# Moving a projection ahead of a transpose, a value projection one step back, a table's second part into two places, and dropping one warm-up product

## Chip, cores and metric

The kernel runs on one core of one Trainium2 chip, as one program. The metric is the device time of the whole execution in microseconds. Three runs of the kernel before gave 546.41, 546.90 and 547.14 us, so the median is 546.90 us.

## The reference, cut to what matters

Everything is float32. There are 8 batches of 256 tokens with 256 features each, and each batch has a context of 120 rows.

```python
# 16 heads of 64; x: (8, 256, 256), context: (8, 120, 256)
q = (layernorm(x) @ w_q);  k, v = context @ w_kv          # 256 -> 1024 each
attn = softmax(q @ k^T / 8)                               # per batch and head, 256 x 120
x = x + tanh(g_xattn) * ((attn @ v) @ w_out + b_out)
# mixture of experts: 8 experts, 256 -> 1024 -> 256, each token goes to its best 2
logits = layernorm(x) @ Wr^T;  gate = top-2 of softmax(logits), divided by their sum
x = x + tanh(g_ffn) * sum_e gate_e * (silu(layernorm(x) @ W1_e^T) @ W2_e^T)
```

## The kernel before, in words

**Order.** The instruction streams of TensorE (PE), VectorE (DVE), ScalarE (ACT) and SyncE (SP) run in the order in which the program text issues them (`tc.manual_schedule`); only GpSimd (POOL) is ordered by a planner. Each engine takes its stream from the front, so an instruction that waits holds up all that is written behind it on the same engine.

**Attention, lines 1067 to 1163.** A loop goes over 32 steps `s`. Step `s` is batch `b`, half of the heads `o`, and half of the tokens `nb`; `k = 2*o + nb` counts the four steps of a batch, and `n = b + 1` is the next batch. In each step the program issues, in this order:

- `scores(s+1)`: 16 small matmuls into `psc` (one pair of PSUM banks, used again by every step), the maximum `mx` on DVE, and eight exponentials on ACT that read `psc`;
- products for this and the next batch: `weigh` (`po`, attention times v), `project_q` (`pq`), `project_v` (`pv`, copied out by ACT), `wide_out` (`pw`), and k for later batches, `project_k` for batch 1 and `project_kk` for two batches at once (`pk`, copied to `kT` by DVE). They take turns in the four PSUM banks of `ps_mm`;
- on DVE the copies of `pk`, and then `divide(s+1)`, the division by the softmax sum;
- in steps with routing the `router`, some twenty short DVE instructions on a 128 by 32 block, with one exponential (L265) on ACT near its start;
- `turn_pr(s)`: eight PE transposes of the divided probabilities into `tr`, copied to `pT_sb` by ACT (L584). The next step's `weigh` reads `pT_sb`.

**Routing in the attention.** When `b` is 3 or 5, the step `k = 1` also computes the logits of the two batches finished before. `logits` issues 16 products into `plT`, a DVE copy to `lgT` (L227), and after a `yield` the PE transpose of `lgT` into `pl` (L230), which the router reads. In step `k = 1` the program issues `plT`, then `project_q`, then that transpose, then `wide_out`, and last `project_kk`. Batch 7 has its own order for this, which is not touched.

**Experts, lines 1182 to 1271.** A loop goes over 31 tiles of 128 rows. Tile `i` issues `go_up` (32 matmuls of `ph`), `open_tile(i+1)` (for gathered tiles a DVE copy of that expert's first weights, L834; then two transposes and the DVE copy `xT`, L856), then on DVE `w2_of()` (for gathered tiles the copy of the second weights, L843), then `close_tile` (16 matmuls `py` of tile `i-1` and its scaling `y` on DVE, L887). The scaled rows are added to the output by an indirect DMA of POOL (L904). The first eight tiles use an expert's weights in place; from tile 8 on, a table built on the chip says which rows and which expert a tile has. That table is the generator `table()`: a first part at `i = 4`, then at `i = 5` the part that gives rows and experts of full tiles (lines 728 to 733, used by the row loads of SP), and at the end of `i = 5` the part for quarter tiles (lines 736 to 782), which also gives `more_i`, a count that every engine loads into a register at `i = 8` (L1198) and that guards a branch at `i = 12` (L1185).

**Start.** Eleven products that nobody reads (`idle`, lines 1048 to 1050) run on PE until the first normalised rows are there.

Of the kernel before, what the change touches and what calls it, by code (L numbers as in the profile page):

```python
# [16 lines left out]
B, N, D = 8, 256, 256  # L17
# [31 lines left out]
def tile_gated_xattn_moe(  # L49
# [232 lines left out]
    def count(n, pool):  # L282

        pc = pool.tile([P, 512], F32, tag="mm", name=f"pc_{n}")
        nc.tensor.matmul(
            pc[:, :E], lhsT=ones, rhs=tally[:, n, :], start=True, stop=True
        )
        return pc[:, :E]
# [202 lines left out]
    def project_kk(b, h):  # L491
# [15 lines left out]
            pk[:, : 4 * M],  # L507
        )

    def project_q(b, xnT, h):  # L510
        pq = ps_mm.tile([P, 2, N], F32, tag="mm", name=f"pq_{b}_{h}")
        for i in range(2):
            for c in range(DC):
                nc.tensor.matmul(  # L514
                    pq[:, i, :],
                    lhsT=wq_sb[:, c, ts(2 * h + i, P)],
                    rhs=xnT[:, c, :],
                    start=(c == 0),
                    stop=(c == DC - 1),
                )  # L520
        nc.scalar.copy(qT_sb[b % 2][:, ts(h, 2), :], pq)

    def project_v(b, j):
        pv = ps_mm.tile([P, 512], F32, tag="mm", name=f"pv_{b}_{j}")
        for c in range(DC):
            nc.tensor.matmul(
                pv[:M, :],
                lhsT=ctxT_sb[:, c, ts(b, M)],
                rhs=wkv_sb[:, c, ds(INNER + j * 512, 512)],
                start=(c == 0),  # L530
                stop=(c == DC - 1),
            )
        nc.scalar.copy(v_sb[b % 2][:, ts(j, 512)], pv[:M, :])
# [152 lines left out]
    def where(first, used, dst):  # L686

        nc.vector.tensor_scalar(first, first, -float(NOWHERE), None, ALU.add)
        nc.vector.tensor_tensor(first, first, used, ALU.mult)
        nc.vector.tensor_scalar(dst, first, float(NOWHERE), None, ALU.add)  # L690
# [8 lines left out]
    def table():  # L699

        rest_i = row("rest_i", E, I32)
        nc.vector.scalar_tensor_tensor(
            rest_i, count(NBLK, fw[2]), float(-P), bump, ALU.add, ALU.add
        )
        whole_i = row("whole_i", E, I32)
        nc.vector.tensor_scalar(whole_i, rest_i, 7, None, ALU.arith_shift_right)
        counts, begin = row("counts", 2 * E), row("begin", 2 * E)
        tails, whole = counts[:, :E], counts[:, E:]  # L710
        nc.vector.tensor_scalar(whole, whole_i, 1.0, None, ALU.mult)
        left = row("left", E)
        nc.vector.scalar_tensor_tensor(
            left, whole, float(-P), rest_i, ALU.mult, ALU.add
        )
        nc.vector.tensor_scalar(tails, left, float(P - QUARTER), None, ALU.is_gt)
        nc.vector.tensor_scalar(begin[:, E:], first_row, float(P), None, ALU.add)
        nc.vector.scalar_tensor_tensor(
            begin[:, :E], whole, float(P), begin[:, E:], ALU.mult, ALU.add
        )  # L720
        upto = summed("w", counts)

        at = row("at", FULLS)
        nc.vector.tensor_scalar(at, places_w, upto[:, 2 * E - 1 :], None, ALU.add)
        used = row("used_w", FULLS)
        nc.vector.tensor_scalar(used, at, 0.0, None, ALU.is_ge)
        yield
        which, first = sought("w", at, upto, counts, begin, P)
        full_row = row("full_row", FULLS, I32)
        where(first, used, full_row)  # L730
        expert_i = row("expert_i", FULLS, I32)
        nc.vector.tensor_scalar(used, which, float(E), float(-E), ALU.is_ge, ALU.mult)
        nc.vector.tensor_tensor(expert_i, which, used, ALU.add)
        yield expert_i, full_row

        quarters = row("quarters", E)
        nc.vector.tensor_scalar(quarters, left, 0.0, None, ALU.is_gt)
        for k in range(1, 3):
            nc.vector.scalar_tensor_tensor(
                quarters, left, float(k * QUARTER), quarters, ALU.is_gt, ALU.add  # L740
            )
        nc.vector.scalar_tensor_tensor(
            quarters, tails, -3.0, quarters, ALU.mult, ALU.add
        )
        upto_q = summed("q", quarters)
        used = row("used_q", 5 * QUADS)
        nc.vector.tensor_scalar(used, places_q, upto_q[:, E - 1 :], None, ALU.is_lt)
        which, first = sought("q", places_q, upto_q, quarters, begin[:, :E], QUARTER)
        where(first, used, first)
        nc.vector.tensor_scalar(which, which, float(E - 1), None, ALU.min)  # L750

        quad_row = row("quad_row", QUADS, I32)
        nc.vector.tensor_scalar(quad_row, first[:, :QUADS], lane, None, ALU.add)
        own = row("own", QUADS * E).rearrange("p (n e) -> p n e", e=E)
        eighth = row("eighth", QUADS)
        nc.vector.tensor_scalar(
            eighth, which[:, :QUADS], -1.0, float(E), ALU.mult, ALU.add
        )
        shape = [P, QUADS, E]
        nc.vector.tensor_tensor(  # L760
            own,
            rank.unsqueeze(1).to_broadcast(shape),
            eighth.unsqueeze(2).to_broadcast(shape),
            ALU.is_equal,
        )
        octets = which[:, QUADS:].rearrange("p (n e) -> p n e", e=E)
        nc.vector.tensor_tensor(
            octets, octets, octal.unsqueeze(1).to_broadcast([P, QUADS // 2, E]), ALU.mult
        )
        experts_i = row("experts_i", QUADS // 2, I32)  # L770
        with nc.allow_low_precision("whole numbers under 2**24, exact"):
            nc.vector.tensor_reduce(experts_i, octets, AX.X, ALU.add)

        more, more_i = row("more", 1), row("more_i", 1, I32)
        nc.vector.tensor_scalar(
            more, upto[:, 2 * E - 1 :], float(SPARE - FULLS), 0.0, ALU.add, ALU.max
        )
        more_q = row("more_q", 1)
        nc.vector.tensor_scalar(
            more_q, upto_q[:, E - 1 :], float(-4 * MIXED), 0.0, ALU.add, ALU.max  # L780
        )
        nc.vector.tensor_tensor(more_i, more, more_q, ALU.add)
        yield quad_row, own, experts_i, more_i

    tables = []
# [260 lines left out]


    idle = ps_tr.tile([P, 4, P], F32, tag="tr", name="idle")
    for _ in range(11):
        nc.tensor.matmul(idle[:, 0, :], lhsT=ones, rhs=before, start=True, stop=True)  # L1050


# [4 lines left out]
    for h in range(2):  # L1057
        project_q(0, xnTs[0], h)
# [8 lines left out]
    for s, (b, o, nb) in enumerate(units):  # L1067
        k = 2 * o + nb
        n = b + 1
# [17 lines left out]
        copies, sums = [], []  # L1087
# [8 lines left out]
                sums.append(wide_out(b - 1, 1, ps_mm))  # L1096
        if k == 0:
            project_q(b, xnTs[b], 3)
            project_v(b, int(b == 0))
        elif n < B:  # L1100
            project_q(n, xnTs[n], k - 1)
        if k == 1:
            if b == 0:
                copies.append(project_k(1, 0))
            if routing and n < B:
                lg = next(lg)
            if b > 0:
                sums.append(wide_out(b - 1, 0, ps_mm))
            if routing and n == B:
                lg = next(lg)  # L1110
        if k == 3:
            if b == 0:
                copies.append(project_k(1, 1))
            if b > 0:
                project_v(b, 1)

        if b == 1:
            copies.append(project_kk(2, k))
        elif 1 < b < 6 and k % 2 == 1:
            copies.append(project_kk(2 * (b // 2) + 2, 2 * (b % 2) + k // 2))  # L1120
        for copy in copies:
            copy()
        if s + 1 < len(units):
# [58 lines left out]
    for i, t in enumerate(order):  # L1182
        if i == 12:

            with tc.If(more > 0):  # L1185
# [8 lines left out]
                    for _ in quad(j, load(("quad", j))):  # L1194
                        pass
                spare = None
        if i == 8:
            more = nc.values_load(tables[1][3][0:1, 0:1], min_val=0, max_val=FULLS)  # L1198
        w2_of = state["ready"][2][2]
        if i == 2:  # L1200
# [12 lines left out]
        copies = []  # L1213
# [10 lines left out]
            open_tile(order[i + 1], xts[i + 1])  # L1224
        if mixed:
            next(running)
        if i == 5:
            tables.append(next(parts))
        if i == 0:
            norms_y.finish()  # L1230
            weigh(B - 1, 1, ps_py)
            load_expert(4)
            turn_y(B - 2, bank_tr)
            sending[g - 1] = places(g - 1, groups[g - 1][0], picked[g - 1], bank_tr)
# [18 lines left out]
        if i == 4:  # L1253
            parts = table()
# [4 lines left out]
                    tc.tile_pool(name="quads", bufs=1, side="right", reuse_waits="tile")  # L1259
                )  # L1260
            )
        if i == 5:
            tables.append(next(parts))
        while len(xts) <= min(i + AHEAD, len(order) - 1 if tables else 7):
            xts[len(xts)] = load(order[len(xts)])
        if i == mix - 4:
# [48 lines left out]
```

## Time and profile before

| what | value |
|---|---|
| median of three runs | 546.90 us |
| the profiled execution, its own time | 546.83 us |
| its span, first to last instruction | 545.1 us |
| mean granted TensorE clock | 0.995 |
| PE busy | 528.0 us, 97% of the span |
| PE weight loads busy | 445.5 us, 82% |
| DVE, ACT, POOL busy | 282.5, 219.6 and 128.7 us |

The busy time of PE runs to a modelled end of each matmul, and matmuls overlap: eight products of `pq` are listed as 1.99 us, but the next group starts 1.83 us after them when nothing is late. So waits of PE are best read as the distance between the starts of two groups, against the same distance elsewhere in the trace. In a list of waits the first number is the idle time of the waiting engine, behind the name of what it waited for. In a timeline the columns are the start, the length, the engine, the line, the operation, the tile written and those read, the shape, the number of instructions merged in the row, and in brackets the idle time just before and what ended it.

### The profile page before, as it was taken

What the parts mean: (1) busy time and instruction counts of PE and PEld (TensorE: products, weight loads), DVE (VectorE), ACT (ScalarE), POOL (GpSimd) and SP (SyncE); (2) the same over time, 40 slices, a digit from 0 to 9 for tenths busy, and PEclk for the clock granted to TensorE, in tenths of its full rate; (3) what the DMA queues carried; (4) which work ended last, traced back from release to release, by engine and by line L of the source; (5) the groups of instructions that cost most, each with busy time, mean ns of one, the idle gap of its engine ahead of it and who ended that gap; (6) DMA issues with size and microseconds to landing.
All of it is one profiled execution on the core that took longest, in us unless ns stands there. A gap on an engine that the chain in (4) does not pass through costs nothing. (4 is left out here: it accounts for less than half of the span.)

```text
span 545.1 us, 9935 instructions
## 1 busy us (share of the span) xinstructions
PE 528.0 (97%) x3700; PEld 445.5 (82%) x3700; DVE 282.5 (52%) x683; ACT 219.6 (40%) x700; POOL 128.7 (24%) x135
## 2 busy tenths in 40 slices
PE   8999999998999999999999999999999999999992
PEld 7788887877878777786789998998997887889991
DVE  3675545664775548655573348344443354443530
ACT  1666546473564634757630310111143645601110
POOL 2011100000332001320003564112331124233422
PEclk9999999999999999999999999999999999999998
DMA  8999991230340500112079932222221220321321
GB/s 298 334 283 280 281 279 44 68 126 2 111 143 30 186 1 20 42 41 59 2 266 321 351 82 71 40 39 34 41 39 31 30 43 6 52 40 15 45 26 19
DMA packets 46439, 57.53 MB, mean 106 GB/s; under 512 B 3184, under 2 KB 41456, under 8 KB 46384
## 3 DMA queue, kind: packets, MB, share of 16 engines
q1 hardware_dynamic: 39488, 47.35, 29.3%
q0 software_dynamic: 6480, 8.81, 9.2%
q8 instruction: 32, 0.52, 0.4%
q10 hardware_dynamic: 416, 0.66, 0.4%
q14 instruction: 23, 0.19, 0.1%
HBM read 28.67 MB, written 28.27 MB: 104 GB/s over the span
## 5 line engine op out<-in xcount | busy, mean ns | idle before, releaser
L564 ACT ACTIVATE pr<-psc,mx 128x120 f32<-128x120 f32 x256 | 88.4, 372 | 69.8 <-DVE mx L558 64.6
L863 PEld LDWEIGHTS ph_full<-xT_full,w 128*128 128x128 f32 x736 | 85.1, 192 | 6.4 <-issue 5.7
L863 PE MATMUL ph_full<-xT_full,w 128*128 128x128 f32 x736 | 86.8, 276 | 0.3 <-PEq L1185 0.3
L879 PE MATMUL py_full<-w,hT_full 128*128 128x256 f32 x368 | 83.1, 379 | 0.0
L879 PEld LDWEIGHTS py_full<-w,hT_full 128*128 128x128 f32 x368 | 68.2, 190 | 8.4
L904 POOL DMA_INDIRECT out_dram<-y_full,xt_full x23 | 40.2, 1746 | 100.8 <-DVE y_full L887 71.8
L514 PE MATMUL pq<-xnT,w_sb 128*128 128x256 f32 x256 | 62.7, 388 | 0.4 <-DVE xnT L207 0.4
L871 ACT ACTIVATE hT_full<-ph_full 128x1024 f32<-128x1024 f32 x23 | 23.5, 1023 | 97.7 <-PE ph_full L863 97.7
L608 PE MATMUL pw<-w_sb 128*128 128x256 f32 x256 | 58.5, 382 | 0.0
L564 ACT ACTIVATION_READ_ACCUMULATOR pr<-psc,mx 128x1 f32 x256 | 55.6, 217 | 0.0
L514 PEld LDWEIGHTS pq<-xnT,w_sb 128*128 128x128 f32 x256 | 46.6, 190 | 10.8 <-issue 1.9
L608 PEld LDWEIGHTS pw<-w_sb 128*128 128x128 f32 x256 | 47.8, 190 | 8.9 <-DVE mx L558 0.8
L552 DVE TENSOR_REDUCE mx<-psc 128x8 f32<-128x960 f32 x32 | 36.8, 1151 | 21.8 <-PE psc L544 21.6
L365 POOL DMA_INDIRECT routed<-rows,slot x32 | 32.2, 1006 | 52.6 <-DVE slot L361 45.6
L584 ACT COPY w_sb<-tr 120x512 f32<-120x512 f32 x64 | 34.8, 603 | 18.2 <-PE tr L583 18.2
L573 DVE TENSOR_TENSOR pr<-pr,sm 128x960 f32<-128x960 f32 x32 | 37.1, 1158 | 1.1
L544 PE MATMUL psc<-kT,w_sb 64*128 64x120 f32 x512 | 37.2, 284 | 0.0
L951 ACT COPY part<-w_sb 128x1024 f32 x32 | 31.1, 1044 | 14.1 <-PE py_q L990 13.5
L544 PEld LDWEIGHTS psc<-kT,w_sb 64*128 64x128 f32 x512 | 31.1, 187 | 6.4 <-issue 3.7
L887 DVE TENSOR_SCALAR y_full<-py_full,gate 128x256 f32<-128x256 f32 x23 | 11.1, 484 | 48.5 <-PE py_full L879 44.8
L593 PE MATMUL po<-w_sb 120*64 120x256 f32 x256 | 32.7, 386 | 2.6 <-ACT w_sb L584 2.6
L583 PE MATMUL tr<-ident,pr 128*120 128x128 f32 x256 | 33.5, 273 | 0.1
(177 smaller groups left out, 664.5 us busy)
## 6 DMA issues: line engine op xcount, KB each, us to landing
routed<-w_sb SPq DMA_DIRECT2D x8, 2120.0 KB, 23.5
w_sb<-in_w1T_dram SPq DMA_DIRECT2D x8, 1024.0 KB, 6.0
w_sb<-in_w2T_dram SPq DMA_DIRECT2D x8, 1024.0 KB, 9.4
xt_full<-routed SPq DMA_DIRECT2D x23, 132.5 KB, 2.1
out_dram<-x SPq DMA_DIRECT2D x8, 256.0 KB, 2.4
x<-in_x_dram SPq DMA_DIRECT2D x7, 256.0 KB, 2.8
w_sb<-in_w_kv_dram SPq DMA_DIRECT2D x3, 512.0 KB, 8.2
xt_first<-routed SPq DMA_DIRECT2D x8, 132.5 KB, 2.7
```

The lines of the kernel that those rows point to most:

```text
L514: nc.tensor.matmul(pq[:, i, :], lhsT=wq_sb[:, c, ts(2 * h + i, P)], rhs=xnT[:, c, :], start=(c == 0), stop=(c == DC - 1),)
L544: nc.tensor.matmul(psc[:, j, ts(i, M)], lhsT=qT[ts(j, DH), 4 * o + i, ts(nb, P)], rhs=kT[ts(j, DH), 4 * o + i, :], start=True, stop=True,)
L552: nc.vector.tensor_reduce(mx.rearrange("p (j i) -> p j i", i=4), psc[:, :, : 4 * M].rearrange("p j (i m) -> p j i m", m=M), AX.X, ALU.max,)
L564: nc.scalar.activation(pr[:, h, :], psc[:, j, ts(i, M)], AF.Exp, bias=mx[:, h : h + 1], scale=QK_SCALE, accum_out=sm[:, h : h + 1],)
L573: nc.vector.tensor_tensor(pr, pr, sm.unsqueeze(2).to_broadcast([P, 8, M]), ALU.mult)
L583: nc.tensor.transpose(tr[:M, i, :], pr[:, 4 * j + i, :], ident)
L584: nc.scalar.copy(pT_sb[:, ts(j, 4), ts(nb, P)], tr[:M, :, :])
L593: nc.tensor.matmul(po[ts(j, DH), k, :], lhsT=v_sb[b % 2][:, ts(2 * (4 * o + i) + j, DH)], rhs=pT_sb[:, 4 * j + i, :], start=True, stop=True,)
L608: nc.tensor.matmul(pw[:, :D], lhsT=oT_sb[b % 2][:, ci, ts(k, P)], rhs=wo_sb[:, ci, :], start=(ci == 0), stop=(ci == IC - 1),)
L863: nc.tensor.matmul(ph[:, f, :], lhsT=w1[:, c, ts(f, P)], rhs=xT[:, c, :], start=(c == 0), stop=(c == DC - 1),)
L879: nc.tensor.matmul(py[:, :D], lhsT=hT[:, f, :], rhs=w2[:, f, :], start=(f == 0), stop=(f == FC - 1),)
L904: add = nc.gpsimd.indirect_dma_start(out=out[:, :], out_offset=bass.IndirectOffsetOnAxis(ap=slots[:, k : k + 1], axis=0), in_=y[own, :], i ...
```

## The change

Four things are done. (1) A helper `next_k` says which k projection belongs to steps `k = 1` and `k = 3`, and these are issued earlier in their step: in `k = 1` ahead of the transpose of the logits and of `wide_out`, in `k = 3` ahead of `project_v`. What is computed in a step stays the same. This concerns batches 1 to 5. (2) The first v projection of the last batch, `project_v(7, 0)`, is issued in the last step of batch 6 behind `project_v(6, 1)`, no longer in the first step of batch 7. (3) The quarter-tile part of the table gets a `yield` in its middle, and its two pieces are issued at `i = 6` and `i = 8`, each behind `open_tile`, instead of at the end of `i = 5`; the register load of `more_i` moves from `i = 8` to `i = 10`. (4) Ten idle products in place of eleven.

```diff
+    def next_k(b, h):
+        if b == 0:
+            return [project_k(1, h)]
+        if b == 1:
+            return [project_kk(2, 2 * h + 1)]
+        if b < B - 2:
+            return [project_kk(2 * (b // 2) + 2, 2 * (b % 2) + h)]
+        return []
...
         where(first, used, first)
+        yield
         nc.vector.tensor_scalar(which, which, float(E - 1), None, ALU.min)
...
-    for _ in range(11):
+    for _ in range(10):
...
             project_q(b, xnTs[b], 3)
-            project_v(b, int(b == 0))
+            if n < B:
+                project_v(b, int(b == 0))
         elif n < B:
             project_q(n, xnTs[n], k - 1)
         if k == 1:
-            if b == 0:
-                copies.append(project_k(1, 0))
+            copies += next_k(b, 0)
             if routing and n < B:
                 lg = next(lg)
...
         if k == 3:
-            if b == 0:
-                copies.append(project_k(1, 1))
+            copies += next_k(b, 1)
             if b > 0:
                 project_v(b, 1)
-
-        if b == 1:
+            if n == B - 1:
+                project_v(n, 0)
+        if b == 1 and k % 2 == 0:
             copies.append(project_kk(2, k))
-        elif 1 < b < 6 and k % 2 == 1:
-            copies.append(project_kk(2 * (b // 2) + 2, 2 * (b % 2) + k // 2))
...
-        if i == 8:
+        if i == 10:
             more = nc.values_load(tables[1][3][0:1, 0:1], min_val=0, max_val=FULLS)
...
-        if i == 5:
+
+        if i in (5, 8):
             tables.append(next(parts))
+        if i == 6:
+            next(parts)
...
-        if i == 5:
-            tables.append(next(parts))
```

## The prediction

> **What bounds the kernel.** I read the page first, then the waits of PE, then the timeline around each place that the change touches.
>
> ```profile
> PE 528.0 (97%) x3700; PEld 445.5 (82%) x3700; DVE 282.5 (52%) x683; ACT 219.6 (40%) x700; POOL 128.7 (24%) x135
> ...
> PE po L593 <- ACT w_sb L584: 2.6, 3, 1.2
> PE idle L1050 <- POOL ones L119: 2.0, 1, 2.0
> PE ph_first L863 <- DVE xT_first L856: 0.9, 1, 0.9
> PE pl L230 <- DVE lgT L227: 0.6, 2, 0.3
> PE pq L514 <- DVE xnT L207: 0.4, 1, 0.4
> PE ph_full L863 <- PEq L1185: 0.3, 1, 0.3
> ```
>
> PE sets the time: it is busy all the way but for a few waits, and what a late wait costs is not won back later. So the change is worth the waits it takes from PE, less those it adds. Rows one, three and four of the waits are the places it touches. The timeline of one routed step (batch 3, k = 1, and the start of k = 2), all engines, rows left out:
>
> ```profile
> 123.76 1.99 PE L514 MATMUL pq<-xnT,w_sb 128*128 128x256 f32 x8
> ...
> 126.06 0.30 PE L230 MATMUL pl<-ident,lgT 128*128 128x128 f32 x1 [0.30 <-DVE lgT L227]
> ...
> 129.65 1.78 PE L498 MATMUL pk<-ctxT_sb,w_sb 128*128 128x240 f32 x8
> ...
> 131.47 0.66 DVE L505 COPY kT<-pk 128x480 f32<-128x480 f32 x1 [5.56 <-PE pk L498]
> ...
> 133.56 0.19 DVE L264 TENSOR_TENSOR p<-pl,lmax 128x32 f32<-128x32 f32 x1
> 133.79 0.23 ACT L265 ACTIVATE p<-p 128x32 f32<-128x32 f32 x1 [5.68 <-DVE p L264]
> 133.93 1.05 ACT L584 COPY w_sb<-tr 120x512 f32<-120x512 f32 x2
> ...
> 134.54 2.43 PE L593 MATMUL po<-w_sb 120*64 120x256 f32 x16 [1.16 <-ACT w_sb L584]
> ```
>
> Two waits hang on one order. The transpose `pl` comes right behind `pq`, before its copy is done. And `pk` comes last, so DVE stands 5.56 us before the copy of `kT`; `divide` and the router are queued behind it; the router's exponential L265 is queued on ACT ahead of the `tr` copies, which are ready long before; and `po` waits for those copies.
>
> **Part 1, k ahead of the turned logits.** Nothing is added. Starts measure the waits. `pq` to its successor is 1.83 us undisturbed (247.74 to 249.57 in batch 6), and 126.06 - 123.76 = 2.30 here: 0.47 lost. In batch 5 it is 196.82 - 194.51 = 2.31: 0.48. `psc` to its successor is 1.08 (122.10 to 123.18), and 2.30 in front of `po` both times (132.24 to 134.54, 203.00 to 205.30): 1.22 each.
>
> New step by step: `pk` starts at 123.76 + 1.83 = 125.59 and takes 1.62 of PE (129.65 to 131.27), so `pl` comes at 127.2; `lgT` was there at 125.91 (125.65 + 0.26), 1.3 early. `pw` runs 3.46 (126.19 to 129.65), so `turn_pr` starts at 130.8 instead of 131.27. On DVE the `kT` copy starts near 127.5 (0.2 behind the last `pk`, as 131.47 is behind 131.27) and ends near 128.15; the step's exponentials ended at 127.63, so `divide` is done near 129.6 and L264 near 130.0, where it was 133.75. L265 is over by 130.4, before `turn_pr` delivers. The `tr` copies then follow PE and end near 132.5; `po` wants them at 131.8 + 1.08 = 132.85. No wait is left. Late next are the maximum of the following step, behind the router on DVE: it moves from about 138.2 to 134.4, so it has more room too. Gain: 0.47 + 0.48 + 1.22 + 1.22 = 3.39.
>
> In the other eight steps (batches 1, 2, 4 and all k = 3) there is no wait of PE to take. In k = 3 v is now behind k, so its ACT copy could push the `tr` copies. The v copies wait for ACT's exponentials anyway: in batch 3 the copy starts at 150.44, the last `pv` ends at 148.34, and 148.34 + 1.62 = 149.96 is still earlier. In batches 1, 2 and 4 the copy moves by 0.3 to 0.6, but `po` starts 0.72 us behind the last `tr` copy there, and that copy moves by 0.1 since it waits for PE's transposes. Cost 0. Without that cover the price is in rival B. The four banks of `ps_mm` rotate in another order; each reuse that I followed finds its reader 1 us or more ahead.
>
> **Part 2, v of batch 7 a step sooner.**
>
> ```profile
> 252.25 1.16 PE L544 MATMUL psc<-kT,w_sb 64*128 64x120 f32 x16
> 253.69 2.43 PE L593 MATMUL po<-w_sb 120*64 120x256 f32 x16 [0.28 <-ACT w_sb L584]
> ```
>
> Here `po` comes 1.44 behind `psc`, 0.36 more than 1.08: ACT finishes its exponentials at 252.19, then copies q, v and `tr` until 254.12. Four `pv` matmuls (257.88 to 259.60, 1.72) move in front of `turn_pr`. `psc` starts at 253.97, `po` wants to start at 255.05. ACT adds one 0.59 copy, from 253.2 to 253.8; the second `tr` copy ends near 254.75. So 0.36 is gained, 0.3 to spare. In the step that loses `pv`, the next `psc` comes at 260.64; it needs the exponentials (near 259.6) and the last q copy (near 260.1). That is enough by 0.5 us. Bounds: -0.3 (q copy late after all) to 0.36. I take 0.36, since each term is a row of the trace.
>
> **Part 3, the table.**
>
> ```profile
> 333.36 3.62 PE L879 MATMUL py_first<-w_sb,hT_first 128*128 128x256 f32 x16
> 337.89 3.84 PE L863 MATMUL ph_first<-xT_first,w_sb 128*128 128x128 f32 x32 [0.91 <-DVE xT_first L856]
> ...
> 331.67 0.16 DVE L737 TENSOR_SCALAR scratch<-scratch 128x8 f32<-128x8 f32 x1
> ...
> 337.41 0.42 DVE L856 COPY xT_first<-xtT_first 128x256 f32<-128x256 f32 x1
> ```
>
> `py` to `ph` is 4.53 us, undisturbed 3.45 (326.12 to 329.57): 1.08 lost, because `xT`, transposed at 333.14, stands behind the quarter part of the table (331.67 to 337.50). In the new order `xT` runs near 333.6; the first piece (L737 to L690 at 336.11 + 0.18, 4.6 us) then runs to 338.6. Queued behind it: `y` of tile 5 (337.75, now 338.6; POOL had been idle 4.9 us before adding it) and the weight copy of tile 8, some 0.8 behind `y` as at tile 10, so 339.5 to 340.7, and its `xT` by 341.3. PE wants both at about 344.1. The second piece (L750 to L782, 1.3 us) goes between `xT` of tile 9 and the copy L843 that ran 349.57 to 350.78: that one ends near 352 and `py` of tile 8 reads it after 355. The next `y` is due at 352.68. The load of `more_i` leaves DVE at i = 8 (0.4 us with its gap) and is paid at i = 10, where the stretch of DVE is as empty; SP's own load (0.27) had waited behind 5 us of buffer waits; POOL's ran at 374.9, far behind, and stays. No DMA moves but the row loads SP issues around it, and those wait for buffers. Gain 1.08; if a piece hits something, 0.5 comes back.
>
> **Part 4, one idle product less.**
>
> ```profile
> 1.95 5.06 PE L1050 MATMUL idle<-before,ones 128*128 128x128 f32 x22 [1.95 <-POOL ones L119]
> ...
> 6.81 0.97 PE L206 MATMUL lnT_a<-ident,xn 128*128 128x128 f32 x4
> ...
> 7.61 1.94 PE L480 MATMUL pk<-ctxT_sb,w_sb 128*128 128x120 f32 x16
> ```
>
> A product is two matmuls of 0.213 us each. Without it PE is free at 6.38; the first normalised rows are done at 6.37, so the transposes start near 6.47, 0.34 sooner. But the transposes run at 0.213 us each and `pk` at 0.112: the clock doubles near 7.55. The Trainium skill, page "TensorE: Matmul & The Clock Gate", section "Part 1: The HAM clock gate", says that the clock rises at the end of a free-running window of activity, by time and not by the number of matmuls. By the row alone all 0.34 stays; by the rule the clock still rises at 7.55, `pk` does its first two matmuls at half speed, and 0.17 stays (14 at 0.112 behind 7.65 end at 9.22 instead of 9.39). If the clock followed the count, 0 would stay. I take 0.17; ends 0 and 0.34.
>
> **Sum.** 3.39 + 0.36 + 1.08 + 0.17 = 5.00. Against the profiled execution: 546.83 - 5.00 = 541.83 (span 540.1, the 1.73 around it kept). The median of the runs is 0.07 above the profiled time, so 541.9.
>
> **Rivals.**
> A. The wait of `po` behind routing stays: the exponential L265 still reaches ACT ahead of late copies, because something else (exponentials, norms) holds `divide`. For: DVE is full there (11.78 of 13.6 us in the stretch from 204.4). Against: DVE stands idle 5.56 us before `kT`. Then 2.44 is not won: 544.3.
> B. Slower: in k = 3 of batches 1 to 5 v's copy on ACT comes a full `pk` (1.62) later and drags the `tr` copies with it. Slacks before `po` are 0.72, 0.72, 0.22, 0.72 and 0.14, so 0.9 + 0.9 + 1.4 + 0.9 + 1.48 = 5.6 would be lost, more than all gains: 547.5. It decides once ACT is free before v is; the trace has ACT busy with exponentials up to the v copy in all five.
> C. Table pieces or the moved v only shift their waits (a later `xT`, the weight copy, the q copy): 1.44 less, 543.3.
>
> **How the numbers follow.** The main case has 0.82, C 0.08, A 0.06; all are faster by over 1.1 us (0.2%, about what a measurement of this kernel can tell from no change). B has 0.02 for slower and 0.02 for about the same, where it bites in part. The main case reaches from 541.0 (0.34 at the start, three runs spread by 0.7, some late copy freed too) to 542.8 (nothing at the start, a 0.5 piece back); the range goes on to 543.5 for C. Faster 0.96, same 0.02, slower 0.02.
>
> **What would show it.** Right: no wait of `pl` on `lgT` in batches 3 and 5; `kT` copies with about 1.6 us of DVE idle before them; 1.08 from `psc` to `po` in three places; 3.45 from `py` to `ph` at tile 7; first transposes near 6.5. Wrong: waits of `po` on L584 at k = 0, a wait of `psc` on ACT in batch 7, a wait of `ph_full` on L834 or of `py_full` on L843 near tile 8 or 9.

## The result and the profile after

The changed kernel takes 540.78 us (median of five runs, 540.71 to 541.29) where the kernel before took 547.14 on the same chip (five runs, 546.41 to 547.95). The ratio is 0.9886, 95% interval 0.9871 to 0.9900: 6.4 us faster. The forecast was 541.9 with a range of 541.0 to 543.5, so the median lies below the range: the direction and the places were right, and the size was too small. The profiled execution took 540.71 with a span of 538.9, so 6.2 us of span are to be explained, and 5.0 were forecast.

The page and the waits of TensorE after (lines behind the new helper have moved down by about ten: L584 is now L594, L593 is L603):

```profile
PE 525.8 (98%) x3698; PEld 444.8 (83%) x3698; DVE 285.1 (53%) x683; ACT 219.8 (41%) x700; POOL 128.7 (24%) x135
...
PE idle L1061 <- POOL ones L119: 2.0, 1, 2.0
PE pq L524 <- DVE xnT L207: 0.4, 1, 0.4
PE ph_full L874 <- PEq L1194: 0.3, 1, 0.3
```

All three waits that the change was read against (`po` on ACT, `ph_first` and `pl` on DVE) are gone from the list. The routed step of batch 3 again, all engines:

```profile
127.17 0.66 DVE L505 COPY kT<-pk 128x480 f32<-128x480 f32 x1 [1.50 <-PE pk L498]
...
129.49 0.23 ACT L265 ACTIVATE p<-p 128x32 f32<-128x32 f32 x1 [1.62 <-DVE p L264]
...
131.23 1.07 ACT L594 COPY w_sb<-tr 120x512 f32<-120x512 f32 x2 [1.51 <-PE tr L593]
131.50 1.16 PE L554 MATMUL psc<-kT,w_sb 64*128 64x120 f32 x16
...
132.59 1.95 PE L603 MATMUL po<-w_sb 120*64 120x256 f32 x16
```

DVE now stands 1.50 us before the copy of `kT`, not 5.56; the router's exponential runs 4.3 us earlier; the `tr` copies wait for nothing but PE; and `po` starts 1.09 behind `psc`. One thing more stands in this view: the `po` group is 1.95 long, where it was 2.43 before.

The two other places, batch 7 and tile 7, after:

```profile
249.32 1.16 PE L554 MATMUL psc<-kT,w_sb 64*128 64x120 f32 x16
250.41 1.95 PE L603 MATMUL po<-w_sb 120*64 120x256 f32 x16
...
328.21 3.62 PE L890 MATMUL py_first<-w_sb,hT_first 128*128 128x256 f32 x16
331.67 3.73 PE L874 MATMUL ph_first<-xT_first,w_sb 128*128 128x128 f32 x32
...
328.41 0.42 DVE L867 COPY xT_first<-xtT_first 128x256 f32<-128x256 f32 x1 [1.80 <-PE xtT_first L865]
```

`po` of batch 7 starts 1.09 behind `psc` and is 1.95 long too. From `py` to `ph` of tile 7 it is 3.46, and `xT` is copied ahead of the table piece.

Because PE runs its groups in a fixed order, the gain can be read at any point as the difference between the starts of the same group in two traces. I use that for every kernel below. "At the first scores" is what the start alone brought.

| stretch | forecast | gain measured |
|---|---|---|
| start, to the first `psc` | 0.17 | 0.25 |
| logits transposed, batches 3 and 5 | 0.47 + 0.48 | 0.49 + 0.50 |
| `psc` to the end of `po`, batches 3 and 5 | 1.22 + 1.22 | 1.71 + 1.70 |
| batch 7, first two steps | 0.36 | 0.84 - 0.33 = 0.51 |
| table, to tile 8 | 1.08 | 1.17 |
| branch behind tile 11 | 0 | -0.05 |
| sum | 5.00 | 6.27 (read at the tiles behind the branch; the rows, rounded, add to 6.28) |

### The profile page after: what moved, and what is told of

Read it like the earlier page. It is cut to its first block, busy times and chain, and to the rows that moved or that the text cites. A ratio compares the mean times of both kernels' runs of the same rounds, so it can differ in the third digit from the quotient of the medians.

```text
span 538.9 us, 9932 instructions
## 1 busy us (share of the span) xinstructions
PE 525.8 (98%) x3698; PEld 444.8 (83%) x3698; DVE 285.1 (53%) x683; ACT 219.8 (41%) x700; POOL 128.7 (24%) x135
## 5 line engine op out<-in xcount | busy, mean ns | idle before, releaser
L915 POOL DMA_INDIRECT out_dram<-y_full,xt_full x23 | 39.0, 1697 | 99.8 <-DVE y_full L898 70.4
L594 ACT COPY w_sb<-tr 120x512 f32<-120x512 f32 x64 | 34.6, 597 | 20.1 <-PE tr L593 20.1
L593 PEld LDWEIGHTS tr<-ident,pr 128*120 128x120 f32 x256 | 29.5, 138 | 5.5 <-issue 2.5
L845 DVE COPY w<-w_sb 128x2048 f32 x23 | 28.8, 1251 | 9.5 <-issue 4.3
## 6 DMA issues: line engine op xcount, KB each, us to landing
xt_full<-routed SPq DMA_DIRECT2D x23, 132.5 KB, 2.1
xt_first<-routed SPq DMA_DIRECT2D x8, 132.5 KB, 2.5
```

The costliest lines, as they stand in the source:

```text
L594: nc.scalar.copy(pT_sb[:, ts(j, 4), ts(nb, P)], tr[:M, :, :])
L915: add = nc.gpsimd.indirect_dma_start(out=out[:, :], out_offset=bass.IndirectOffsetOnAxis(ap=slots[:, k : k + 1], axis=0), in_=y[own, :], i ...
```

## Experiments

Times of one group of kernels come from one chip; a difference of a few tenths of a microsecond is read from the traces, since the times of one kernel spread by 1 us and more.

**Each part alone.** Four kernels, each the kernel before with one part of the change.

```diff
# k_only: next_k, and the calls of project_k / project_kk that it replaces
# v_only
             project_q(b, xnTs[b], 3)
-            project_v(b, int(b == 0))
+            if n < B:
+                project_v(b, int(b == 0))
...
+            if n == B - 1:
+                project_v(n, 0)
# table_only: the yield, the calls at i = 6 and 8, the register load at i = 10
# idle_only
-    for _ in range(11):
+    for _ in range(10):
```

> The kernel before with part 1 alone (k ahead of the turned logits and of v). Theory 1: in front of the attention-times-v products stood two waits in a row, one for the first and one for the second copy of the turned probabilities, and both go: per routed step 0.49 at the logits, 1.22 ahead of the products and 0.48 inside their group, so 2 x 2.19 = 4.4 us faster than before. Rival: only the waits that the prediction counted belong to this part (3.39 us) and the 1 us above it comes from the other parts, or from the parts together.

Measured: 542.81 against 546.92, ratio 0.9927 (0.9907 to 0.9948). In the trace the gain grows from 0.36 at the first scores to 4.76 behind batch 5: 4.40, in four steps of 0.49, 1.70, 0.50 and 1.71. Theory 1 holds, and its rival falls: the whole 4.4 belongs to this part. At the branch behind tile 11 this trace gives back 0.25 of it (from 4.75 to 4.50). The other traces give back between 0 and 0.47 there, and no experiment looked for the reason.

> The kernel before with part 2 alone (first v of the last batch one step sooner). Theory 1: the wait of the products on both copies goes (0.36 + 0.48 = 0.84), and the logits of the last batch get a new wait of 0.33 on the copy of the turned rows, which stands on VectorE behind the division that waits for ScalarE's exponentials: 0.5 us faster. Rival: the new wait comes from the earlier start of the step and is not there without the other parts: 0.84. Prediction: 0.36.

Measured: 546.67, ratio 0.9999 (0.9992 to 1.0005), too small for the times. The trace: 0.06 ahead of the place, 0.88 one step behind it, 0.56 two steps behind it, and 0.56 still at the first expert tile. So 0.82 comes and 0.32 goes back, without any other part: theory 1. Where it goes back is in the changed kernel's own timeline:

```profile
254.90 0.20 DVE L582 RECIPROCAL sm<-sm 128x8 f32<-128x8 f32 x1 [1.03 <-ACT pr L574]
255.13 1.16 DVE L583 TENSOR_TENSOR pr<-pr,sm 128x960 f32<-128x960 f32 x1
...
256.21 0.69 DVE L207 COPY xn2T<-lnT_f 128x512 f32<-128x512 f32 x1
256.61 0.97 PE L219 MATMUL plT<-xn2T,wr_sb 128*32 128x128 f32 x16
...
256.94 0.36 PEld L219 LDWEIGHTS plT<-xn2T,wr_sb 128*32 128x32 f32 x12 [0.20 <-DVE xn2T L207]
```

PE reaches the logits of batch 7 sooner, because the step ahead lost 1.72 us of `pv`. Their input `xn2T` is copied by DVE behind the division (254.90 and 255.13), which waits for ACT's exponentials, and those end as long behind the scores they read as before (5.5 and 5.6 us behind the start of `psc`). The first four products run, the other twelve wait: 0.97 for the group instead of 0.64.

> The kernel before with part 3 alone (quarter part of the table in two pieces at tiles 6 and 8, register load at tile 10). Theory 1: 1.08 of wait plus 0.10 of slow restart in the group behind it: 1.15 to 1.2 us faster. Rival: the pieces only do no harm because tile 5 comes 5 us earlier by the other parts; alone the gathered tiles 8 and 9 wait for their weight copies and less than 0.8 is left.

Measured: 545.82, ratio 0.9980 (0.9973 to 0.9987), so 1.1 us. The trace: 0.48 ahead of tile 7 and 1.66 at tile 8, that is 1.18. Theory 1; the part does not lean on the others.

> The kernel before with part 4 alone (ten idle products). Theory 1: the first transposes start 0.34 sooner, the clock rises at its own time, 0.25 us is left at the first scores, and nothing downstream takes it back: 0.25 us faster, at the edge of what can be measured. Rival: the clock follows the number of matmuls, 0; or the rise of the clock is at another time in other executions, so that the executions differ by 0.3 among themselves.

Measured: 546.89, ratio 0.9999 (0.9988 to 1.0011), and in its trace the first scores come 0.14 later than in the kernel before. The row shows why:

```profile
1.96 4.63 PE L1050 MATMUL idle<-before,ones 128*128 128x128 f32 x20 [1.96 <-POOL ones L119]
6.49 1.11 PE L206 MATMUL lnT_a<-ident,xn 128*128 128x128 f32 x4
7.40 2.29 PE L480 MATMUL pk<-ctxT_sb,w_sb 128*128 128x120 f32 x16
```

The transposes start 0.32 sooner than with eleven products, but `pk` takes 2.29 where it took 1.94, since in this execution the clock rose at 8.1 us. Theory 1 is half right: the transposes do start sooner, but the clock does not rise at one fixed time; it differs between executions by more than the edit is worth, as the rival's second half has it. Over the traces with ten products the first scores lie between 0.14 later and 0.40 sooner than in the trace of before; over the other traces with eleven, between 0.09 later and 0.47 sooner. No gain of part 4 can be told from that. The clock is not all of this spread: in v_only, router_behind and k_first `pk` also waits 0.18 to 0.22 us for the DMA of its weights. In v_only and table_only the clock rises at the same time (6.29 and 6.26), and the first scores still come at 12.88 and 12.48.

**The chain behind the wait of `po`.** Two kernels keep PE's order of before and cut one link each.

```diff
# copy_behind: in the routed steps, DVE copies kT behind division and router
-        for copy in copies:
-            copy()
+        held = routing and n < B and k == 1
+        if not held:
+            for copy in copies:
+                copy()
...
             picked[g] = router(g, lg)
+        if held:
+            for copy in copies:
+                copy()
# router_behind: the router is issued behind the transposes
-        if routing and n < B and k == 1:
-            picked[g] = router(g, lg)
...
         turn_pr((b, o, nb), *prs.pop(s))
+        if routing and n < B and k == 1:
+            picked[g] = router(g, lg)
```

> The kernel before with TensorE's order kept, but in the two routed steps VectorE copies kT behind the division and the router, not ahead of them. Theory 1 (the wait of the attention-times-v products came from VectorE standing at the kT copy with division and router queued behind it): the two waits of 1.22 and the 0.48 inside the group go, the wait of the transpose on the logits' copy stays: 2 x 1.70 = 3.4 us faster. Rival: it is the place of the k products on TensorE that matters (they fill it while ScalarE is late): no change, or the wait moves on.

Measured: 543.63 against 547.09, ratio 0.9932 (0.9911 to 0.9953). The gain in the trace is 1.70 in each routed step, 3.4 in all, and the wait of `pl` on `lgT` is still there (0.47 goes back at the branch behind tile 11).

```profile
129.30 0.23 ACT L265 ACTIVATE p<-p 128x32 f32<-128x32 f32 x1 [1.31 <-DVE p L264]
...
129.52 1.78 PE L498 MATMUL pk<-ctxT_sb,w_sb 128*128 128x240 f32 x8
...
133.16 0.65 DVE L505 COPY kT<-pk 128x480 f32<-128x480 f32 x1
133.20 1.95 PE L593 MATMUL po<-w_sb 120*64 120x256 f32 x16
```

`pk` is as late on PE as before, and `po` starts in time all the same. So the place of `pk` on PE was not by itself what held `po`: DVE standing at the copy, with division and router behind it, was.

> The kernel before with all of the router issued behind the transposes of the probabilities in the two routed steps; the kT copy still waits for the late k products. Theory 1 (the last link is the router's exponential queued on ScalarE ahead of the copies of the turned probabilities): 3.4 us faster, the same as with the copy moved, although VectorE still stands 5.6 us at the kT copy. Rival: VectorE's lateness itself, not ScalarE's order, holds the products: no gain.

Measured: 546.55, ratio 0.9991 (0.9982 to 0.9999). Neither theory: the gain behind the first routed step is 0.88, and two steps on only 0.19 of it is left; at the second routed step it is 0.50, of which 0.11 is left. The timeline of that kernel:

```profile
131.56 0.66 DVE L505 COPY kT<-pk 128x480 f32<-128x480 f32 x1 [5.56 <-PE pk L498]
...
132.05 1.07 ACT L584 COPY w_sb<-tr 120x512 f32<-120x512 f32 x2 [3.86 <-PE tr L583]
...
133.41 1.95 PE L593 MATMUL po<-w_sb 120*64 120x256 f32 x16
...
134.26 0.23 ACT L265 ACTIVATE p<-p 128x32 f32<-128x32 f32 x1 [1.14 <-DVE p L264]
...
140.58 1.25 DVE L600 COPY w_sb<-po 128x512 f32<-128x512 f32 x2
141.30 0.41 PE L317 MATMUL pp<-both,before 128*128 128x32 f32 x2 [0.56 <-DVE w_sb L600]
```

The last link was read rightly: with L265 behind the copies on ACT, `po` starts 1.09 behind `psc` and its group takes 1.95. But DVE is as late as before. Its copy of `po` comes at 140.58, 7 us behind the start of the products, and the product `pp`, which by the row waits for that copy (it takes its bank from the same four), waits in turn. Two steps on the next `po` has both of its waits again: it starts 1.29 behind `psc` and is 2.43 long, which is where 0.69 goes back. The change frees DVE 4 us earlier and has no such wait.

**Which steps matter.**

```diff
# k_two_steps: the changed kernel, next_k kept for b = 3 and 5 in k = 1 alone
-        if b == 1:
-            return [project_kk(2, 2 * h + 1)]
-        if b < B - 2:
+        if b in (3, 5) and h == 0:
             return [project_kk(2 * (b // 2) + 2, 2 * (b % 2) + h)]
...
-        if b == 1 and k % 2 == 0:
+        if b == 1:
             copies.append(project_kk(2, k))
+        elif 1 < b < 6 and k % 2 == 1 and not (k == 1 and b in (3, 5)):
+            copies.append(project_kk(2 * (b // 2) + 2, 2 * (b % 2) + k // 2))
```

> The changed kernel with the earlier k kept only in the two routed steps (batches 3 and 5, second step); batches 1, 2, 4 and all fourth steps as before. Theory 1: the same time as the changed kernel, 540.8, within 0.2. Rival: the other eight steps carry a part of the 1.3 us that the prediction missed, then 541.1 to 542.

Measured: 541.14 against 547.09, ratio 0.9903 (0.9871 to 0.9934). By its four times alone (540.77 to 543.73) the median would be in the rival's range, so the trace has to decide. It gains 0.50, 1.70, 0.50 and 1.70 in the two steps, within 0.01 of the changed kernel, and in the other eight steps neither trace moves. They are worth nothing, as forecast.

**What is left.**

```diff
# turn_first: the changed kernel, DVE copies the turned rows of batch 7 ahead of the division
+        if k == 0 and n == B:
+            turn_y(b - 2, bank_mm)
         if s + 1 < len(units):
             divide(*prs[s + 1])
-        if k == 0 and b > 1:
+        if k == 0 and 1 < b < B - 1:
             turn_y(b - 2, bank_mm)
```

> The changed kernel with one thing more: in the first step of the last batch VectorE copies the turned rows ahead of the division, not behind it. Theory 1: the new wait of 0.33 inside the logits' products goes, and the division comes 0.3 later without anyone waiting: 540.45. Rival: the division's reader or the next maximum becomes late: 540.8 or more.

Measured: 540.29 against 547.09, ratio 0.9874 (0.9854 to 0.9893). The new wait is gone:

```profile
254.63 0.69 DVE L207 COPY xn2T<-lnT_f 128x512 f32<-128x512 f32 x1 [0.90 <-PE lnT_f L206]
...
255.46 1.16 DVE L583 TENSOR_TENSOR pr<-pr,sm 128x960 f32<-128x960 f32 x1
...
256.48 0.64 PE L219 MATMUL plT<-xn2T,wr_sb 128*32 128x128 f32 x16
```

The logits take 0.64 again, and nothing is given back. This is the fastest kernel of the study; its 0.3 over the change is shown by the trace, not by the times, whose intervals overlap.

The next three ran on a chip whose times spread more (the kernel before took 548.49 there, 546.72 to 551.93), so their traces carry the reading.

```diff
# table_whole: the changed kernel without the yield, the whole quarter part at i = 6
-        if i in (5, 8):
+        if i in (5, 6):
             tables.append(next(parts))
-        if i == 6:
-            next(parts)
```

> The changed kernel with the quarter part of the table undivided, all of it (5.9 us of VectorE) at tile 6 behind the copy of the turned rows. Theory 1 (the gain of part 3 is the move behind that copy; the split only spreads the load): the part ends about 1.3 us later than the first piece did, the weight copy of tile 8 with it, and TensorE wants that 2.8 us after its end, so 540.8 as the changed kernel. Rival: the split is needed, tile 8 waits for its weights or its turned rows and 0.3 to 1.3 us come back.

Measured: 541.58, ratio 0.9860 (0.9809 to 0.9911). Against the trace of before the gain falls from 5.26 at tile 5 to 4.93 at tile 6 and 4.82 one group on, and then rises to 5.89 at tile 7 and 6.00 at tile 8. The rise of 1.18 is that of the changed kernel (5.15 to 6.32, 1.17), and no wait of tile 8 or 9 appears: the gain of part 3 is the place behind the copy of `xT`, and the split bought nothing here. The loss of 0.44 ahead of it is something else. DVE copies `xT` of tile 6 only at 324.17, 3 us behind its transposes, and the table is written behind that copy. The traces of the next two kernels, which have the split, lose 0.27 at the same tile. The cause stays open.

```diff
# idle_7: the changed kernel with seven idle products
-    for _ in range(10):
+    for _ in range(7):
```

> The changed kernel with seven idle products, not ten: TensorE is free at about 5.1 us and idle until the first normalised rows at about 6.4. Theory 1 (the clock rises by time, anywhere between 6.2 and 8.2 us after the start in the executions so far, whatever the number of products; the transposes wait for the rows): 540.8 within the spread of the starts, 0.3. Rival: the pause of over a microsecond counts against the clock[...]: 1 to 1.7 us slower.

Measured: 542.73 (seven runs, 540.42 to 545.04), ratio 0.9890 (0.9851 to 0.9929). The rival was right for the profiled execution, and the cost was a little above its 1.7:

```profile
1.95 3.35 PE L1061 MATMUL idle<-before,ones 128*128 128x128 f32 x14 [1.95 <-POOL ones L119]
6.53 1.12 PE L206 MATMUL lnT_a<-ident,xn 128*128 128x128 f32 x4 [1.22 <-DVE xn L196]
7.43 3.61 PE L480 MATMUL pk<-ctxT_sb,w_sb 128*128 128x120 f32 x16
```

After a pause of 1.22 us, `pk` runs its whole length at 0.213 us a matmul (3.61 against 1.96), and the granted clock rises only at 11.5 us (the first clock record of that trace). The first scores come 2.05 later than in the changed kernel.

```diff
# k_first: turn_first, and in batch 0 the k products of batch 1 ahead of the q products
         elif n < B:
+            if b == 0 and k == 1:
+                copies += next_k(b, 0)
             project_q(n, xnTs[n], k - 1)
```

> The changed kernel with the turned rows copied ahead of the division in batch 7 and one order more: in the second step of batch 0 the k products for batch 1 go ahead of the q products, which wait there 0.4 us (0.62 behind their place) for the copy of the turned rows. Theory 1: 0.6 us more than with the copy alone, near 539.7. Rival: the q copy on ScalarE becomes late for the next scores and the wait moves there: 540.3.

Measured: 541.90, ratio 0.9867 (0.9814 to 0.9921). The wait of `pq` on `xnT` is gone from PE's list. In the changed kernel `pq` stood 0.49 behind its place (27.11 against 25.54 + 1.08), not the 0.62 of the expectation; 0.35 of this is won at the next scores, but 0.33 goes back one group on:

```profile
31.45 1.16 PE L554 MATMUL psc<-kT,w_sb 64*128 64x120 f32 x16
32.53 2.30 PE L603 MATMUL po<-w_sb 120*64 120x256 f32 x16
...
31.71 1.13 ACT L594 COPY w_sb<-tr 120x512 f32<-120x512 f32 x2
```

The `po` group takes 2.30 here and 1.97 in the changed kernel: it starts at 32.53, and the second copy of the probabilities on ACT ends at 32.84 (31.71 + 1.13). In the changed kernel that copy ends at 32.75 and `po` starts at 32.77, so ACT is the bound in batch 0. A later `po` is 0.10 shorter, so 0.12 is left in all. The rival was right that the wait moves, though not to the q copy that it named.

## Where the prediction was right, and the step that failed

- **Part 1, the places and the chain: right.** `pl` at 126.97 (forecast 127.2, less 0.24 from the start), `kT` copied at 127.17 (127.5), division done at 129.13 (129.6), the next maximum at 133.75 (134.4). The copies of `tr` end at 132.30 (132.5), and no wait is left.
- **Part 1, the size: wrong, and this is the step that failed.** The prediction took "`psc` to its successor" (2.30 against 1.08) for all of the wait in front of `po`. It measured the start of the group and not its length. The group waits twice: half of its products need the first copy of `tr`, the others the second. The trace of before had the second wait on the weight loads:

```profile
134.54 0.19 PEld L593 LDWEIGHTS po<-w_sb 120*64 120x64 f32 x2 [1.34 <-ACT w_sb L584]
135.03 1.49 PEld L593 LDWEIGHTS po<-w_sb 120*64 120x64 f32 x14 [0.30 <-ACT w_sb L584]
```

  Two weight loads at 134.54, the other fourteen at 135.03, behind the end of the second copy (133.93 + 1.05 = 134.98). PE's own row did not show it, because a group is drawn as busy from its first start to its last end: 2.43 against 1.95 undisturbed. The term measured 1.70 per routed step and not 1.22. The same term was missed in part 2, where the prediction's own figures held it: `tr` is copied until 254.12, and `po` starts at 253.69. That is 0.48 three times, 1.45 us in all, more than the whole error of 1.27. For the other steps the prediction did compare the start of `po` with the end of the last copy; in the three places where it counted a gain it looked, for the order of before, at the start of `po` alone.
- **Part 2: the sum near, the terms not.** 0.84 instead of 0.36, by the same second wait; and 0.33 given back at the logits. That 0.51 came near 0.36 is luck: two missed terms of opposite sign. A loss of 0.3 stood in the bounds of this part, but for another reason (the q copy, which ended in time at 255.34). The prediction had not followed that DVE copies the turned rows behind a division paced by ACT.
- **Part 3: right.** 1.07 at tile 7 for 1.08, and 0.10 more since the group that waited had also been slow itself (3.68 from start to start against 3.57). Both pieces found the room that was forecast: the weight copy of tile 8 ended at 336.0, and PE's first use came at 338.91. That room was wide enough for the undivided part too.
- **Part 4: not shown.** The 0.25 seen in one pair of executions is within what the start does by itself, so it is chance that it lies near the forecast 0.17. The rule taken from the Trainium skill ("TensorE: Matmul & The Clock Gate", section "Part 1: The HAM clock gate"), that the clock rises by a free-running window of activity and not by a count, is in part borne out: the clock rose between 6.3 and 8.1 us, with ten products and with eleven, and 20 to 28 matmuls had started by then, so it is no count. That a free-running window sets the moment no run here shows. The prediction erred in holding the 7.55 of one execution fixed.
- **Rivals.** A (the wait of `po` stays), B (slower by v's copy in the fourth steps) and C (waits only shift) did not come true as wholes; C was true for 0.33 in batch 7. B's price needed ACT to be free before v, and `k_two_steps` shows that the fourth steps move nothing.
- **Sum.** 5.00 + 1.45 (second waits) + 0.04 (logits of batches 3 and 5) - 0.33 (logits of batch 7) + 0.09 (table) + 0.08 (start) - 0.05 (branch) = 6.28, against 6.27 read at the tiles behind the branch.

## What to carry to other kernels

When an engine waits in front of a group of instructions, compare the length of the group with an undisturbed one as well: a group with two inputs can wait a second time inside itself, and the busy rows hide it. A wait of the bounding engine can be ordered by a queue two engines away; find the instruction that stands first there, and either feed it sooner or write it last. When work is taken out of a step, follow what the next step reads from the engines that did not get faster.

## What the runs showed of the hardware

- The moment at which TensorE's clock doubles (starts of `pk`'s matmuls 0.213 us apart before it, 0.112 behind it) moved between 6.3 and 8.1 us among executions with ten or eleven idle products. In the two extreme traces, table_only and idle_only, the first scores are 0.61 us apart, and both traces keep that distance up to tile 6. A DMA wait of about 0.2 us in three of the traces adds to the spread. So an edit at the start cannot be judged from one pair of executions.
- In the one trace taken with a pause of 1.22 us between the idle products and the first real work, the rise came at 11.5 us, and the first scores came 2.05 us later than in the changed kernel. Of that kernel's seven executions the fastest took 540.42, about what the changed kernel takes, so the pause does not always seem to cost this; what decides was not measured further.
